# Six tile buffers instead of four, a last row tile turned by TensorE, and a check moved into the next layer, in a two-layer graph kernel

## The chip, the core and the metric

The kernel runs on one core of one Trainium2 chip. The metric is the device time of one execution in microseconds (us). The time before is the median of 3 runs.

## What is computed

The graph has 3327 nodes with 256 features each. Layer 0 does two steps. In each, it multiplies the features by a row-normalised `adj + I`, and, beside that, by a top-p attention matrix made from the features. Layer 1 is a graph attention with four heads, masked by `adj > 0`. Everything is float32. Cut to what matters here:

```
# layer 0, twice (Xa and Xf start as h = relu(layernorm(x)))
probs = softmax((Xa W1' W2') (Xa W3')')            # 3327 x 3327
keep  = the largest probs of a row until their sum reaches 0.9
A     = probs * keep, each row divided by its sum
Xf    = R Xf            # R = adj + I, rows divided by their sums
Xa    = A Xa
Z    += Xf U1[n]' + Xa U2[n]'
x = x + layernorm(h + Z)
# layer 1
hp    = relu(layernorm(x)) W                        # 4 heads of 64
attn  = softmax over j of leaky_relu(s_i + d_j), where adj[i, j] > 0
x = x + elu(attn hp)
```

## The kernel before, in words

**Tiles.** The 3327 rows are padded to 26 tiles of 128 (`NT`). In each of the two steps every tile t has two large jobs on TensorE (PE):

- The *row* job makes row tile t of the attention matrix and multiplies it. PE makes the logits (L906), ScalarE (ACT) takes their exponentials (L921), and ACT, GpSimd (POOL) and VectorE (DVE) search the threshold of each row: counting passes on ACT (L958), arithmetic on single columns on POOL (L960 to L1006), the window, sort and choice on DVE (`window`, `sort`, `choose`, L1008 to L1066). DVE then zeroes what falls below the threshold in three parts (`drop`, L1072). PE needs the row tile turned (the 128 nodes of j on the partitions). That is done in three stages: DVE turns 32 x 32 blocks (`turn_blocks`, L1084), SyncE (SP) issues a DMA that puts a part into the DRAM tensor `blocks` (`put_blocks`, L1088), and four DMAs fetch it back with the blocks in their new places (`get_blocks`, L1093). PE multiplies (`attend_blocks`, L1100, 26 products into the one bank `acca`), and ACT takes the result out (`attended`, L1104). In step 2, `finish2` carries the row on through two layer norms to layer 1's `hp`.
- The *full* job multiplies tile t of `adj + I`. SP loads it in seven pieces of up to four 128 x 128 tiles (`Full.load`, L1119) into the buffers called `at`, of which there are four. POOL adds the identity to the one diagonal tile (L1132), PE multiplies (`some`, L1125, into the one bank `accf`), and ACT or DVE takes the result out.

**Layer 1** goes over four blocks of 832 columns, and in each over j = 0 to 25. SP loads the tiles of `adj` for one j into two `at` buffers (L1680), ACT makes a 0/1 mask of them (L1690, L1691), DVE makes four lots of masked exponents (L1702), PE multiplies (L1718) and sums (L1732). The exponents of j = 3, 10 and so on lie in the room of `c`, those of j = 5 and 6 in that of `rhs`. So the first can't be written before all full jobs of step 2 are done, the second not before all row jobs are. In block 0 the sums (L1732) wait for all row jobs, since they use the same two banks.

**What sets the order.** Nothing is scheduled on the chip: each engine's queue runs in program order. That order is laid out by a planner while the program is built (`Plan`, L471). Each piece of work is put into it with an engine, a duration, a *rank* (the lowest goes first among those that are ready), what it needs, buffers that it takes and gives back by name, and a *lag*: how long after its end its result is counted as there. A DMA's lag stands for its flight time. The planner runs through these numbers and writes down who goes when; a wrong lag gives no wrong result, it only puts an instruction at a place in its queue where it then waits. Six of these numbers belong to the change: the lags of `put_blocks` (8.0) and `get_blocks` (5.5) at L1527 and L1530, that of `Full.load` (4.0) at L1544, the rank of step 2's full jobs (`base + 1.0 + t`, L1969, where row jobs have `base + t`), the rank of `failures` (L1973), and the buffer counts at L867.

**`failures`** (L1439) is a chain of small DVE instructions over one column per tile. It notes rows for which the search failed. `judge` reads it at the very end, and the program runs a slow general version of everything if any did. No row of the profile belongs to that version.

**Room.** SBUF is full, so a buffer more here is one less elsewhere. The pool `et` has three buffers of 2048 bytes per partition. They hold small weights at the start, copies for `stats` (L826), layer 1's vectors and their products (L757, L766), and in layer 1 the masks (L1685).

Of the kernel before, what the change touches and what calls it, by code (L numbers as in the profile page):

```python
# [10 lines left out]
F32 = mybir.dt.float32  # L11
BF16 = mybir.dt.bfloat16
# [3 lines left out]
ALU = mybir.AluOpType  # L16
# [3 lines left out]
P = 128  # L20
# [26 lines left out]
PIECES = 16  # L47
PART = 1024
PIECE_AT = [PART * (k // 5) + 205 * (k % 5) for k in range(PIECES)] + [N]
QUANTILE = (6.4004942, -10.1694914, 9.3637353, -4.4723851)  # L50

REACH = 40.0

BUFS = dict(kk=2, e=4, sc=6, f=3, xa=2, xt=2, kq=3, ystage=2, base=1, mv=4, cum=2)

# [531 lines left out]
def fast(  # L587
# [58 lines left out]
    with ExitStack() as l0:  # L646
        wpool = l0.enter_context(tc.tile_pool(name="wpool", bufs=1))
        small = l0.enter_context(tc.tile_pool(name="small", bufs=2))
        epool = l0.enter_context(tc.tile_pool(name="epool", bufs=4))
        apool = l0.enter_context(tc.tile_pool(name="apool", bufs=4))  # L650
        etpool = l0.enter_context(tc.tile_pool(name="etpool", bufs=3))
        scr = l0.enter_context(tc.tile_pool(name="scr", bufs=1))
# [24 lines left out]

        small.tile([P, 8], F32, name="room", bufs=1)
        stat = wpool.tile([P, 2, NT], F32, name="stat")
# [20 lines left out]
        def weights():  # L700
            held = {}
            w1 = etpool.tile([P, 4, P], F32, name="et")
            w1 = w1[:, 0, :].rearrange("p (c o) -> p c o", c=2)
# [48 lines left out]
        def layer1_loads():  # L752

            late = wpool.tile([P, 2 * D + 2 * (H * FH + 2 * H)], F32, name="late")
            g_all, b_all = late[:, :D], late[:, D : 2 * D]
            wa = late[:, 2 * D :].rearrange("p (c o) -> p c o", c=2)
            a_all = etpool.tile([P, H, 2 * FH], F32, name="et")  # L757
            nc.sync.dma_start(g_all, ln_g.partition_broadcast(P))
            nc.sync.dma_start(b_all, ln_b.partition_broadcast(P))
            nc.sync.dma_start(a_all, gat_a.partition_broadcast(P))  # L760
            nc.sync.dma_start(wa[:, :, : H * FH], gat_w.rearrange("(c p) o -> p c o", p=P))
            return g_all, b_all, wa, a_all

        def layer1_scores(wa, a_all):

            prod = etpool.tile([P, 2, H, FH], F32, name="et")  # L766
            for k in range(2):
                for a in range(2):
                    V.tensor_mul(
                        prod[:, 0],  # L770
                        wa[:, k, : H * FH].rearrange("p (h f) -> p h f", h=H),
                        a_all[:, :, a * FH : (a + 1) * FH],
                    )
                    lo = H * FH + a * H
                    V.tensor_reduce(wa[:, k, lo : lo + H], prod[:, 0], AX.X, ALU.add)

# [34 lines left out]
        def stats(n, lo, hi, rank, needs, scaled):  # L811
# [13 lines left out]
            def copy(held, m):  # L825
                qg = etpool.tile([P, 4, P], F32, name="et").rearrange("p a b -> p (a b)")  # L826
                held["qg"] = qg[:, : 3 * (2 * DA + 1)].rearrange("p (a b) -> p a b", a=3)
                S.copy(held["qg"][:, :m, :], held["ps"][:, :m, :])
# [10 lines left out]
            for t0 in range(lo, hi, 2):  # L839
                held, m = {}, min(2, hi - t0)  # L840
                a = plan.put("PE", 0.25 * m, rank, product, held, t0, m, needs=[needs, scaled], take=["px"])
                a = plan.put("ACT", 0.45, rank, copy, held, m, needs=[a], take=["et"], give=["px"])
                ends.append(plan.put("DVE", 0.35 * m + 0.2, rank, square, held, t0, m, needs=[a], give=["et"]))

# [21 lines left out]

        plan = Plan(dict(rows=1, mvs=3, pl=2, px=2, acca=1, accf=1, et=3, at=4, y=1, e2=2, ec=1, mask=2, e5=1, qg=2, **BUFS))  # L867
        own_e = [[("e", "e5")[i % 5 == 2 - n] for i in range(NT)] for n in range(STEPS)]
# [3 lines left out]
        class Row:  # L872
# [42 lines left out]
            def exps(self, k):  # L915
                pl = self.pl.pop(k)
                to, m = self.e[:, PART * k : min(PART * (k + 1), NP)], pl.shape[1]
                sums = (self.p0, self.p1, self.p2, self.p3)
                to = to.rearrange("p (g q t) -> p g t q", q=P, t=2)
                if k < 3:  # L920
                    S.activation(to, pl.rearrange("p (g t q) -> p g t q", g=4, t=2), AF.Exp, accum_out=sums[k])  # L921
                else:
                    S.activation(to[:, 0, 0, :], pl[:, :P], AF.Exp, accum_out=self.p3)
                    S.activation(to[:, 0, 1, : m - P], pl[:, P:], AF.Exp, accum_out=self.p4)

            def row_sum(self):
                k = self.NAMES.index("p4")
                S.activation(self.sc[:, k + 5 : k + 10], self.sc[:, k : k + 5], AF.Copy, accum_out=self.s)

# [144 lines left out]
            def total(self):  # L1074

                GP.tensor_scalar(self.v, self.all, self.zs, self.rec, ALU.subtract, ALU.add)
                GP.tensor_tensor(self.rec, self.v, powers[:, 2:3], ALU.pow)

            def part(self, g):
# [440 lines left out]
        def attention(row, rank, total, drops, right):  # L1520
            a = None
            come = []
            for g in range(3):
                b = plan.put(
                    "DVE", 1.17 if g < 2 else 1.44, rank - 1.001, row.turn_blocks, g, needs=[drops[g]]
                )
                b = plan.put("SP", 0.5, rank - 1.0, row.put_blocks, g, needs=[b], lag=8.0)  # L1527
                b = plan.put("", 0.0, -90.0, lambda: None, needs=[b], lag=0.0)
                come.append(
                    [plan.put("SP", 0.6, rank - 1.0, row.get_blocks, g, o, needs=[b], lag=5.5) for o in range(4)]  # L1530
                )
            for j in range(0, NT - 2, 4):
                js = range(j, j + 4 if j < 20 else NT)
                a = plan.put(
                    "PE", 0.432 * len(js), rank, row.attend_blocks, js, needs=[come[j // 8], a, right],
                    take=["acca"] * (j == 0), give=[own_e[row.n][row.i]] * (j == 20),
                )
            return plan.put("ACT", 0.4, rank - 2.7, row.attended, needs=[a, total], take=["xa"], give=["acca", "sc"])

        def full(n, t, rank, right, after):  # L1540

            f = Full(n, t)
            loads = [
                plan.put("SP", 0.4, rank, f.load, q, needs=[after], take=["at"], lag=4.0) for q in range(-(-NT // JC))  # L1544
            ]
# [19 lines left out]
        def attend_neighbours(rows, ends, done, fulls):  # L1565
# [80 lines left out]
            for b in range(4):  # L1646
# [11 lines left out]

                seen, last_acc, last_den, last_e = [], None, None, None
                group, halves = [], [None, None]  # L1660
                for j in range(NT):
# [21 lines left out]

                    def mask(held=held, off=off):
                        m = etpool.tile([P, 4, P], F32, name="et").rearrange("p a b -> p (a b)").bitcast(BF16)  # L1685
                        m = held["mask"] = m[:, :W]
                        A, B = (held.pop(g).rearrange("p i q -> p (i q)") for g in range(2))
                        A, B = A[:, off:], B[:, : W + off - 4 * P]
                        for to, src in ((m[:, : 4 * P - off], A), (m[:, 4 * P - off :], B)):
                            S.activation(src, src, AF.Relu)  # L1690
                            S.activation(to, src, AF.Sign)  # L1691
# [48 lines left out]

                    own = ["et", "mask"]
                    if b == 0 and j < 2:
                        loads, own = plan.put("SP", 0.2, rank, load_first, needs=[opened[0]], lag=4.0), []
                        m_ = plan.put("ACT", 1.8, rank, mask_first, needs=[loads])
                    else:
# [3 lines left out]
                        ]  # L1749
                        m_ = plan.put("ACT", 2.2, rank, mask, needs=[loads], take=own, give=["at", "at"])  # L1750
                    mine = ("e", "e", "e", "ec", "e", "e2", "e2")[j % 7]
# [191 lines left out]
        for n in range(STEPS):  # L1943
# [22 lines left out]
            if n == 0:  # L1966
                drawn[0] = rows[-1].pieces["logits"]
            fulls = [
                full(n, t, (2.0 + 1.3 * t if n == 0 else base + 1.0 + t), [p[0] for p in sources], [p[1] for p in sources] if n == 0 else loaded[0])  # L1969
                for t in range(NT)  # L1970
            ]
            done = [attention(r, base + r.i, *found[r.i], right) for r in rows]
            failed.append(plan.put("DVE", 2.95, base + NT, failures, n, needs=[[a for a, _ in found]]))  # L1973
            if n == 0:
# [21 lines left out]
                def layer1():  # L1996
# [6 lines left out]
                layer1_ready = plan.put(  # L2003
                    "DVE", 3.7, base + 5.0, lambda: layer1_scores(late["wa"], late["a"]), needs=[a], take=["et"],
                    give=["et", "et"],
                )
# [74 lines left out]
```

## Time and profile before

| what | value |
|---|---|
| median of 3 runs | 2075.99 us (2071.98 to 2077.3) |
| the profiled execution, whole | 2077.04 us |
| its span in the profile | 2075.2 us |
| DVE busy | 1696.3 us (82%) |
| ACT busy | 1298.7 us (63%) |
| POOL busy | 1040.1 us (50%) |
| DMA moved | 361.61 MB, mean 174 GB/s |
| granted clock of PE, mean | 0.992 |

The profiled execution is 1.05 us longer than the median, and 1.84 us of it lie around the span. The stages follow each other like this in the trace: preparation to about 100 us; step 1 to about 790 us, where the first logits of step 2 are made, while full jobs of step 1 run on to 909 us; step 2 to about 1600 us; layer 1 to the end.

How to read the lines below. A line of a PE timeline gives the start, the time from there to the end of a run of like instructions, the line of the program, the output and inputs, the number of records, and in brackets how long PE had been idle before it and who released it. One product of 128 x 128 with 256 columns makes two records. The ends of matmuls are modelled, so neighbouring pieces overlap by some tenths. A line of a table by stages gives the stretch, its length, then for each engine the busy time and in parentheses the number of its instructions, then the granted clock of PE (1.00 is full speed), the busy share of the DMA engines, and GB/s.

### The profile page before, as it was taken

The page shows a single profiled execution, that of the slowest core. Times are in us where ns is not written, and L with a number is a line of the kernel's source. Part 1 is how long each engine was busy: PE and PEld are TensorE (multiplying, and loading weights), DVE is VectorE, ACT ScalarE, POOL GpSimd, SP SyncE. Part 2 cuts the span into 40 slices and gives each one's busy share as a digit, 9 for nine tenths or more (in the row PEclk, how much of TensorE's full clock was granted, in tenths as well). Part 3 has the DMA queues.
Part 4 walks back from the last instruction along what each step waited for, and adds up shares of the span by engine and source line. Part 5 has one row for each costly group of instructions (what it writes and reads, how often), then busy time and mean ns, then how long its engine had stood idle before and what let it go on. Part 6 is the DMA issues. An engine that isn't in the chain of part 4 may idle for free. (4 is left out here: it accounts for less than half of the span.)

```text
span 2075.2 us, 33982 instructions
## 1 busy us (share of the span) xinstructions
PE 2025.6 (98%) x10519; PEld 1401.3 (68%) x10519; DVE 1696.3 (82%) x3768; ACT 1298.7 (63%) x2630; POOL 1040.1 (50%) x2222
## 2 busy tenths in 40 slices
PE   8999999999999999999999999999998999999997
PEld 6477777878787776788888788778876333333332
DVE  5479989887997742888679888898888999999894
ACT  4677685677756405884677777877643456474642
POOL 5367676665765503787576777878771000000001
PEclk9999999999999999999999999999999999999999
DMA  3177677776786756687757777676786444444440
GB/s 96 38 209 192 188 203 216 194 196 190 198 220 193 209 151 181 199 220 216 196 156 216 202 199 201 192 206 184 214 251 200 117 132 140 140 132 116 117 123 26
DMA packets 637551, 361.61 MB, mean 174 GB/s; under 512 B 373706, under 2 KB 590320, under 8 KB 637360
## 3 DMA queue, kind: packets, MB, share of 16 engines
q1 hardware_dynamic: 636464, 359.13, 61.9%
q8 instruction: 86, 1.41, 0.3%
q14 instruction: 105, 0.86, 0.1%
q10 hardware_dynamic: 896, 0.21, 0.0%
HBM read 254.39 MB, written 104.58 MB: 173 GB/s over the span
## 5 line engine op out<-in xcount | busy, mean ns | idle before, releaser
L1100 PE MATMUL acca<-rhs,e 128*128 128x256 f32 x2184 | 485.6, 380 | 4.1 <-DMA e<-blocks 2.3
L958 ACT ACTIVATE junk<-e,sc 128x3327 fp8e5<-128x3327 f32 x147 | 450.8, 3066 | 39.7 <-POOL sc L995 38.2
L1100 PEld LDWEIGHTS acca<-rhs,e 128*128 128x128 f32 x2184 | 427.9, 197 | 49.4 <-issue 3.5
L1125 PE MATMUL accf<-main,at 128*128 128x257 f32 x1352 | 323.8, 389 | 14.1 <-DMA at<-in_adjt_dram 7.6
L1125 PE MATMUL accf<-c,at 128*128 128x256 f32 x1352 | 308.6, 382 | 5.9 <-DMA at<-in_adjt_dram 2.2
L1125 PEld LDWEIGHTS accf<-main,at 128*128 128x128 f32 x1352 | 253.4, 193 | 76.6 <-issue 19.0
L1125 PEld LDWEIGHTS accf<-c,at 128*128 128x128 f32 x1352 | 252.4, 190 | 57.1 <-issue 8.9
L1021 DVE MAX8 cands<-y 128x8 f32<-128x205 f32 (+1 forms) x832 | 242.7, 362 | 3.7
L1016 DVE SCALAR_TENSOR_TENSOR y<-e,sc 128x1639 f32<-128x1639 f32 x84 | 167.5, 1994 | 65.4 <-POOL sc L1006 64.4
L1881 POOL TENSOR_TENSOR qq<-qq 128x256 f32<-128x256 f32 x4 | 2.9, 730 | 431.6 <-ACT qq L1877 431.5
L1691 ACT ACTIVATE et<-at 128x448 bf16<-128x448 f32 (+1 forms) x204 | 112.2, 550 | 128.6 <-DVE e L1702 73.4
L1718 PE MATMUL pl<-e,main 128*64 128x416 f32 x1024 | 191.6, 517 | 0.0
L921 ACT ACTIVATE e<-pl 128x1024 f32<-128x1024 f32 x126 | 137.8, 1101 | 64.5 <-PE pl L906 54.7
L906 PE MATMUL pl<-kt,qg 64*128 64x512 f32 (+1 forms) x832 | 174.0, 536 | 2.4 <-ACT e L921 2.4
L1084 DVE STREAM_TRANSPOSE e<-e 128x1024 f32<-128x1024 f32 (+1 forms) x126 | 168.7, 1339 | 7.1 <-DVE e L1072 0.5
L1072 DVE SCALAR_TENSOR_TENSOR e<-e,thr 128x1024 f32<-128x1024 f32 (+1 forms) x126 | 170.7, 1354 | 1.5 <-issue 0.4
L1718 PEld LDWEIGHTS pl<-e,main 128*64 128x64 f32 x1024 | 69.3, 137 | 109.8 <-issue 93.7
L1690 ACT ACTIVATE at<-at 128x448 f32<-128x448 f32 (+1 forms) x204 | 110.6, 542 | 45.5 <-DMA at<-in_adjt_dram 45.4
L1702 DVE SCALAR_TENSOR_TENSOR e<-c,low,et 128x832 f32<-128x832 f32 x128 | 129.4, 1071 | 8.1 <-issue 6.2
L906 PEld LDWEIGHTS pl<-kt,qg 64*128 64x128 f32 x832 | 71.4, 186 | 88.3 <-issue 74.1
L1702 DVE SCALAR_TENSOR_TENSOR e<-qq,low,et 128x832 f32<-128x832 f32 x120 | 121.4, 1076 | 8.2 <-ACT at L1690 4.3
L1104 ACT ACTIVATE xa<-acca,sc 128x256 f32<-128x256 f32 x52 | 24.3, 467 | 151.3 <-PE acca L1100 151.2
(547 smaller groups left out, 3454.2 us busy)
## 6 DMA issues: line engine op xcount, KB each, us to landing
at<-in_adjt_dram SPq DMA_DIRECT2D x414, 256.0 KB
blocks<-e SPq DMA_DIRECT2D x84, 512.0 KB
e<-blocks SPq DMA_DIRECT2D x336, 128.0 KB
blocks<-e SPq DMA_DIRECT2D x42, 640.0 KB
e<-blocks SPq DMA_DIRECT2D x168, 160.0 KB
at<-in_adjt_dram SPq DMA_DIRECT2D x102, 192.0 KB
blocks<-qq SPq DMA_DIRECT2D x20, 512.0 KB
qq<-blocks SPq DMA_DIRECT2D x80, 128.0 KB
```

The source lines that it names most:

```text
L906: T.matmul(pl[:, lo : lo + m], qg[self.n, self.i // 4][half, self.i % 4, :], kt[half, 512 * k : 512 * k + m], start=True, stop=True,)
L921: S.activation(to, pl.rearrange("p (g t q) -> p g t q", g=4, t=2), AF.Exp, accum_out=sums[k])
L958: S.activation(junk[:, :N], self.e[:, :N], fn, bias=t, scale=-1.0, accum_out=dst, saturate=False)
L1016: V.scalar_tensor_tensor(self.y[:, : hi - lo], self.e[:, lo:hi], self.up, self.e[:, lo:hi], ALU.is_lt, ALU.mult, accum_out=(self.h0, self. ...
L1021: V.max(self.cands[:, a * PIECES // 2 + k, :], self.y[:, at[k] - lo : at[k + 1] - lo])
L1072: V.scalar_tensor_tensor(piece, piece, self.thr[:, at : at + 1], piece, ALU.is_gt, ALU.mult)
L1084: V.transpose(part, part)
L1100: T.matmul(self.acc, lhs, rhs[self.n][:, j, :], start=(j == 0), stop=(j == NT - 1))
L1125: T.matmul(self.acc[:, : self.w], self.at[j // JC][:, j % JC, :], self.src[:, j, : self.w], start=(j == 0), stop=(j == NT - 1),)
L1691: S.activation(to, src, AF.Sign)
L1702: V.scalar_tensor_tensor(held["e"][:, k, :], extra["both"][b % 2][:, k, :], low[:, j, k : k + 1], held["mask"], ALU.max, ALU.mult,)
L1718: T.matmul(q["acc"][a][k * FH : (k + 1) * FH, c, :C], main[:, j, h * FH : (h + 1) * FH], held["e"][:, h, c * C : (c + 1) * C], start=(j == 0),
```

## The change

The change has these parts.

1. **Buffers.** `at` gets six buffers of 2048 bytes for four. The room comes from `et`, which shrinks to one buffer of 3072 bytes, and from `f`, which has two for three. `stats` now uses `f` for its copies, layer 1's vectors and their products share the one `et`, and the masks of layer 1 lie in two halves of the room called `m` (that of `junk`), where only the first two lay before.
2. **The last row tile of step 2** (tile 25 of the second step, and no other) takes another way. Its exponentials are stored in plain order. PE turns it in seven groups of up to four 128 x 128 tiles into PSUM (`turn`), ACT or DVE copies each group into an `at` buffer (`turned`), and PE multiplies from there (`attend`). This row has no `turn_blocks`, `put_blocks` or `get_blocks`.
3. **`failures` of step 2** gets rank 63.0 where it had `base + NT`, which is 56. Layer 1's block 0 has ranks from 60 on.
4. **Planner numbers.** The lag of `put_blocks` is 7.0 for 8.0, of `get_blocks` 5.0 for 5.5, of `Full.load` 5.5 for 4.0. The full jobs of step 2 have rank `base + 2.0 + 1.05 * t` for `base + 1.0 + t`.

```diff
+BLOCKED = (NT, NT - 1)
...
-BUFS = dict(kk=2, e=4, sc=6, f=3, xa=2, xt=2, kq=3, ystage=2, base=1, mv=4, cum=2)
+BUFS = dict(kk=2, e=4, sc=6, f=2, xa=2, xt=2, kq=3, ystage=2, base=1, mv=4, cum=2)
...
-        apool = l0.enter_context(tc.tile_pool(name="apool", bufs=4))
-        etpool = l0.enter_context(tc.tile_pool(name="etpool", bufs=3))
+        apool = l0.enter_context(tc.tile_pool(name="apool", bufs=6))
+        etpool = l0.enter_context(tc.tile_pool(name="etpool", bufs=1))
...
-                qg = etpool.tile([P, 4, P], F32, name="et").rearrange("p a b -> p (a b)")
-                held["qg"] = qg[:, : 3 * (2 * DA + 1)].rearrange("p (a b) -> p a b", a=3)
+                qg = small.tile([P, H * FH + 2 * H], F32, name="f", bufs=BUFS["f"])
+                held["qg"] = qg[:, : 2 * (2 * DA + 1)].rearrange("p (a b) -> p a b", a=2)
...
-        plan = Plan(dict(rows=1, mvs=3, pl=2, px=2, acca=1, accf=1, et=3, at=4, y=1, e2=2, ec=1, mask=2, e5=1, qg=2, **BUFS))
+        plan = Plan(dict(rows=1, mvs=3, pl=2, px=2, acca=1, accf=1, et=1, at=6, y=1, e2=2, ec=1, mask=2, e5=1, qg=2, **BUFS))
...
-                if k < 3:
+                if self.i >= BLOCKED[self.n]:
+                    S.activation(self.e[:, PART * k : PART * k + m], pl, AF.Exp, accum_out=sums[k])
+                elif k < 3:
...
+            def turn(self, g):
+                m = min(4, NT - 4 * g)
+                pt = self.pt[g] = ps_x.tile([P, 4, P], F32, name="px")
+                for k in range(m):
+                    j = 4 * g + k
+                    T.transpose(pt[:, k, :], self.e[:, j * P : (j + 1) * P], ident)
...
+            def turned(self, g, copy):
+                m = min(4, NT - 4 * g)
+                self.et[g] = apool.tile([P, JC, P], F32, name="at")
+                copy(self.et[g][:, :m, :], self.pt.pop(g)[:, :m, :])
+
+            def attend(self, g):
+                if g == 0:
+                    self.acc = ps_a.tile([P, D], F32, name="acca")
+                et = self.et.pop(g)
+                for j in range(4 * g, min(4 * g + 4, NT)):
+                    T.matmul(
+                        self.acc, et[:, j - 4 * g, :], rhs[self.n][:, j, :], start=(j == 0), stop=(j == NT - 1)
+                    )
...
+            if row.i >= BLOCKED[row.n]:
+                for g in range(GROUPS):
+                    m = min(4, NT - 4 * g)
+                    b = plan.put(
+                        "PE", 0.11 * m, rank - 0.01 * (GROUPS - g), row.turn, g, needs=[drops[min(((4 * g + m) * P - 1) // PART, 2)]],
+                        take=["px"], give=[own_e[row.n][row.i]] * (g == GROUPS - 1),
+                    )
+                    b = plan.either(
+                        ("ACT", 0.06 + 0.105 * m, row.turned_by_s), ("DVE", 0.12 + 0.135 * m, row.turned_by_v),
+                        rank - 2.6, g, needs=[b], take=["at"], give=["px"],
+                    )
+                    a = plan.put(
+                        "PE", 0.432 * m, rank, row.attend, g, needs=[b, a, right], take=["acca"] * (g == 0), give=["at"]
+                    )
+                return plan.put("ACT", 0.4, rank - 2.7, row.attended, needs=[a, total], take=["xa"], give=["acca", "sc"])
...
-                b = plan.put("SP", 0.5, rank - 1.0, row.put_blocks, g, needs=[b], lag=8.0)
+                b = plan.put("SP", 0.5, rank - 1.0, row.put_blocks, g, needs=[b], lag=7.0)
...
-                    [plan.put("SP", 0.6, rank - 1.0, row.get_blocks, g, o, needs=[b], lag=5.5) for o in range(4)]
+                    [plan.put("SP", 0.6, rank - 1.0, row.get_blocks, g, o, needs=[b], lag=5.0) for o in range(4)]
...
-                plan.put("SP", 0.4, rank, f.load, q, needs=[after], take=["at"], lag=4.0) for q in range(-(-NT // JC))
+                plan.put("SP", 0.4, rank, f.load, q, needs=[after], take=["at"], lag=5.5) for q in range(-(-NT // JC))
...
-                    def mask(held=held, off=off):
-                        m = etpool.tile([P, 4, P], F32, name="et").rearrange("p a b -> p (a b)").bitcast(BF16)
-                        m = held["mask"] = m[:, :W]
+                    def mask(j=j, held=held, off=off):
+                        m = held["mask"] = extra["m"][:, j % 2, :]
...
-                        m_ = plan.put("ACT", 2.2, rank, mask, needs=[loads], take=own, give=["at", "at"])
+                        m_ = last_m = plan.put("ACT", 2.2, rank, mask, needs=[loads, last_m], take=own, give=["at", "at"])
...
-                full(n, t, (2.0 + 1.3 * t if n == 0 else base + 1.0 + t), [p[0] for p in sources], [p[1] for p in sources] if n == 0 else loaded[0])
+                full(n, t, (2.0 + 1.3 * t if n == 0 else base + 2.0 + 1.05 * t), [p[0] for p in sources], [p[1] for p in sources] if n == 0 else loaded[0])
...
-            failed.append(plan.put("DVE", 2.95, base + NT, failures, n, needs=[[a for a, _ in found]]))
+            failed.append(plan.put("DVE", 2.95, base + NT if n == 0 else 63.0, failures, n, needs=[[a for a, _ in found]]))
```

More of the change, by code (lines that the diff above doesn't have):

```diff
@@ L676, in fast @@
             GP.tensor_copy(gk[:DA, DA + 1 :], ident[:DA, :DA])
-        small.tile([P, 8], F32, name="room", bufs=1)
+        small.tile([P, 16], F32, name="room", bufs=1)
         stat = wpool.tile([P, 2, NT], F32, name="stat")
@@ L701, in weights @@
             held = {}
-            w1 = etpool.tile([P, 4, P], F32, name="et")
+            w1 = etpool.tile([P, 3 * D], F32, name="et")[:, : 4 * P].rearrange("p (a b) -> p a b", a=4)
             w1 = w1[:, 0, :].rearrange("p (c o) -> p c o", c=2)
@@ L756, in layer1_loads @@
             wa = late[:, 2 * D :].rearrange("p (c o) -> p c o", c=2)
-            a_all = etpool.tile([P, H, 2 * FH], F32, name="et")
+            a_all = etpool.tile([P, 3 * D], F32, name="et")
+            prod = a_all[:, 2 * D :].rearrange("p (h f) -> p h f", h=H)
+            a_all = a_all[:, : 2 * D].rearrange("p (h f) -> p h f", h=H)
             nc.sync.dma_start(g_all, ln_g.partition_broadcast(P))
@@ L761, in layer1_loads @@
             nc.sync.dma_start(wa[:, :, : H * FH], gat_w.rearrange("(c p) o -> p c o", p=P))
-            return g_all, b_all, wa, a_all
+            return g_all, b_all, wa, (a_all, prod)
         def layer1_scores(wa, a_all):
-            prod = etpool.tile([P, 2, H, FH], F32, name="et")
+            a_all, prod = a_all
             for k in range(2):
@@ L769, in layer1_scores @@
                     V.tensor_mul(
-                        prod[:, 0],
+                        prod,
                         wa[:, k, : H * FH].rearrange("p (h f) -> p h f", h=H),
@@ L774, in layer1_scores @@
                     lo = H * FH + a * H
-                    V.tensor_reduce(wa[:, k, lo : lo + H], prod[:, 0], AX.X, ALU.add)
+                    V.tensor_reduce(wa[:, k, lo : lo + H], prod, AX.X, ALU.add)
         def moments(n, t, kq, ps_k, ps_g):
@@ L841, in stats @@
                 a = plan.put("PE", 0.25 * m, rank, product, held, t0, m, needs=[needs, scaled], take=["px"])
-                a = plan.put("ACT", 0.45, rank, copy, held, m, needs=[a], take=["et"], give=["px"])
-                ends.append(plan.put("DVE", 0.35 * m + 0.2, rank, square, held, t0, m, needs=[a], give=["et"]))
+                a = plan.put("ACT", 0.45, rank, copy, held, m, needs=[a], take=["f"], give=["px"])
+                ends.append(plan.put("DVE", 0.35 * m + 0.2, rank, square, held, t0, m, needs=[a], give=["f"]))
             def variance():
@@ L926, in row_sum @@
             def row_sum(self):
-                k = self.NAMES.index("p4")
-                S.activation(self.sc[:, k + 5 : k + 10], self.sc[:, k : k + 5], AF.Copy, accum_out=self.s)
+                m = 5 if self.i < BLOCKED[self.n] else 4
+                k = self.NAMES.index("p0") + 1
+                S.activation(self.sc[:, k + 5 - m : k + 5], self.sc[:, k - m : k], AF.Copy, accum_out=self.s)
             def root(self):
@@ L1077, in total, with turned_by_s, turned_by_v @@
                 GP.tensor_tensor(self.rec, self.v, powers[:, 2:3], ALU.pow)
+            def turn(self, g):
[4 more added lines that the diff above has]
+                    T.transpose(pt[:, k, :], self.e[:, j * P : (j + 1) * P], ident)
+            def turned_by_s(self, g):
+                self.turned(g, S.copy)
+            def turned_by_v(self, g):
+                self.turned(g, V.tensor_copy)
+            def turned(self, g, copy):
[10 more added lines that the diff above has]
+                    )
             def part(self, g):
@@ L1657, in open_den @@
                     q["den"] = [ps_a.tile([P, 512], F32, name=n) for n in ("acca", "accf")]
-                seen, last_acc, last_den, last_e = [], None, None, None
+                seen, last_acc, last_den, last_e, last_m = [], None, None, None, None
                 group, halves = [], [None, None]
@@ L1739, in sums @@
                                 )
-                    own = ["et", "mask"]
+                    own = ["mask"]
                     if b == 0 and j < 2:
-                        loads, own = plan.put("SP", 0.2, rank, load_first, needs=[opened[0]], lag=4.0), []
-                        m_ = plan.put("ACT", 1.8, rank, mask_first, needs=[loads])
+                        loads = plan.put("SP", 0.2, rank, load_first, needs=[opened[0]], lag=4.0)
+                        m_ = last_m = plan.put("ACT", 1.8, rank, mask_first, needs=[loads, last_m], take=own)
                     else:
@@ L2003, in fast @@
                 layer1_ready = plan.put(
-                    "DVE", 3.7, base + 5.0, lambda: layer1_scores(late["wa"], late["a"]), needs=[a], take=["et"],
-                    give=["et", "et"],
+                    "DVE", 3.7, base + 5.0, lambda: layer1_scores(late["wa"], late["a"]), needs=[a], give=["et"],
                 )
```

## The prediction

> **What bounds the kernel now.** I read the page first, then a table by stages, then PE's timeline around each stage where PE was not full, then what the other engines did there.
>
> ```profile
> PE 2025.6 (98%) x10519; PEld 1401.3 (68%) x10519; DVE 1696.3 (82%) x3768; ACT 1298.7 (63%) x2630; POOL 1040.1 (50%) x2222
> PE   8999999999999999999999999999998999999997
> ```
>
> PE is the bound: 49.6 us of 2075.2 are idle. No part of the change takes work from PE, so the most it can win is idle time and what follows from it. The table says where that is:
>
> ```profile
> 0.00:101.00 101.00, 90.73 (x384) 55.02 (x385) 50.72 (x191) 59.04 (x150) 42.49 (x136) 0.97 0.23 66
> ...
> 700.00:800.00 100.00, 89.94 (x390) 72.93 (x389) 45.71 (x137) 18.75 (x36) 19.98 (x41) 0.95 0.65 180
> ...
> 1150.00:1500.00 350.00, 345.88 (x1607) 281.67 (x1606) 302.62 (x766) 264.60 (x509) 275.91 (x591) 1.00 0.73 199
> 1500.00:1605.00 105.00, 94.48 (x441) 73.53 (x441) 88.83 (x192) 47.06 (x91) 53.59 (x96) 0.97 0.79 228
> 1605.00:2020.00 415.00, 415.00 (x3033) 151.78 (x3031) 394.53 (x450) 231.14 (x564) 3.74 (x3) 1.00 0.44 127
> 2020.00:2076.00 56.00, 44.60 (x314) 13.77 (x309) 27.52 (x41) 13.11 (x30) 5.34 (x7) 0.92 0.11 32
> ```
>
> The head (10.3) and the tail (about 10.6 to the end of the span) are not touched. Layer 1 has no PE idle time at all. What is left are two passages: from step 1 to step 2 (10.1 idle in 700 to 800, clock 0.95) and from step 2 to layer 1 (10.5 in 1500 to 1605, clock 0.97), and some 7 us scattered elsewhere. PE's timeline names the waits:
>
> ```profile
> 748.45 2.01 PE L1125 MATMUL accf<-main,at 128*128 128x257 f32 x8 [0.73 <-DMA at<-in_adjt_dram]
> 753.11 3.69 PE L1125 MATMUL accf<-main,at 128*128 128x257 f32 x8 [2.66 <-DMA at<-in_adjt_dram]
> 756.63 11.39 PE L1100 MATMUL acca<-rhs,e 128*128 128x256 f32 x52
> ...
> 785.54 5.40 PE L1125 MATMUL accf<-main,at 128*128 128x257 f32 x12 [4.17 <-DMA at<-in_adjt_dram]
> ```
>
> ```profile
> 1519.47 0.70 PE L1125 MATMUL accf<-c,at 128*128 128x256 f32 x2 [2.15 <-POOL at L1132]
> 1521.29 3.58 PE L1100 MATMUL acca<-rhs,e 128*128 128x256 f32 x8 [1.12 <-DVE y L1016]
> ...
> 1588.71 4.48 PE L1100 MATMUL acca<-rhs,e 128*128 128x256 f32 x20
> 1593.12 1.62 PE L1718 MATMUL pl<-e,main 128*64 128x416 f32 x8
> 1599.27 1.30 PE L1732 MATMUL acca<-e,qd 128*32 128x416 f32 x8 [4.54 <-ACT xa L1104]
> ```
>
> Eight records of L1125 take 2.01 us, but 3.69 after the gap at 753: the gap costs twice, once idle and once in a slow clock (granted 0.50 to 0.57 from 753 to 756, 0.50 from 784 to 790 in slices of 1 us).
>
> **Part 1, six `at` buffers (passage 1).** A buffer is 4 tiles of work: 1.75 us of PE (11.39 for 26). Four hold 7.0, six 10.5, so 3.5 more. Whether the two more would be full is read from the stretch ahead: PE spends 724 to 736 and 757 to 768 on a row job (52 records each), which frees no `at` buffer, and in 5 us slices the DMA share falls to 0.12 and 0.31 (730 to 740), and 0.01 and 0.03 (760 to 770), with SP's next load held back by PE (L1119 <- PE accf, 18.7 us in 700 to 800). So the two loads fall into idle DMA time and push nothing. They cover 0.73 + 2.66 whole and 3.5 of the 4.17: 6.9. Clock: 3.69 against 2.01 is 1.7; 12 records in 5.40 against 2.88 is 2.5; together 4.2.
>
> Here the Trainium skill, "TensorE: Matmul & The Clock Gate" (Part 1), would give less: it says that the clock halves after an idle window of about 3.4 us. By that rule only the 4.17 gap pays (2.5). The rows show that 2.66, and 2.15 and 1.12 with 0.7 of work between, pay too, so I use the rows. Full gain 6.9 + 4.2 = 11.1. Bounds 0 (the row's twelve fetches, which have DMA at a share of 1.0 from 745 to 757, are what binds) and 12. I take 8, since part of the work moved forward meets the next wait, such as a fetch of `rhs`.
>
> The same buffers cover the scattered waits for tiles in step 2 (1.34, 0.35 and 0.22): 1.5.
>
> **What pays for the buffers.** `f` and `et` lose one and two. `stats` is 13 copies per step, each held until a DVE instruction is done, about 1 us; a full job's copy of step 1 that met two of them would hold `accf` by that. PE waits for that copy 1.7 us in all now; bounds 0 and +2, taken 0.5. The masks lose nothing: two were allowed before (`mask`=2), two halves are there now. A half is written while the other is read; that parts of one buffer don't wait for each other is seen at 1535 to 1541, where DVE goes on with parts 1 and 2 of a row while the put of part 0 is in flight.
>
> **Part 2, the last row by TensorE (passage 2).** Removed: three turns on DVE (1.25 + 1.25 + 1.52 = 4.0), three puts and twelve gets, whose issues take 11.2 us of SP's queue (0.38, 0.39, 0.46; 4.62, 2.37, 2.94) and move 3.3 MB, 14.6 us of DMA at this stage's 228 GB/s. Added: 26 transposes and seven copies of 512 columns. Two transposes of L1401 stand 0.22 apart from what follows, so 26 are 2.9 us, and PE is the bound, so they count whole. The skill speaks against this one: the same page (Part 4, PE-mode transpose) says that full clock does not engage for transposes and that they don't count as busy. By that they would take 5.7 and leave PE slow behind. The start of this trace says otherwise:
>
> ```profile
> 1.79 4.14 PE L1922 MATMUL accf<-ident 128*128 128x128 f32 x19 [1.79 <-POOL ident masks.py:199]
> 5.77 0.43 PE L1211 MATMUL pl<-ident,rhs 128*128 128x128 f32 x2
> 6.03 0.82 PE L1922 MATMUL accf<-ident 128*128 128x128 f32 x6
> ```
>
> All of these are transposes: 0.218 each at first, 0.11 to 0.14 after 4 us of nothing else. They do raise the clock. I take 2.9 (bounds 2.9 and 5.7). The copies: 0.37 for 256 columns (ACT, L1405) makes an estimated 0.65 for 512, 4.5 in all, on an ACT that waits 11.04 us at 1564 and is busy 47 of 105 here; taken at nothing, at worst 0.7 per group not overlapped, 4.5. The plain exponentials are four ACT instructions of 1.1 us as before (bounds -0.3 and +0.3).
>
> What it wins: the last drop ends at 1568.5, or about 1566 without the turns between, and PE now begins the last row at 1579.7 and its last part at 1588.7. With seven groups of 0.44 (PE) and 0.65 (ACT), the whole row is there by about 1569. PE gets it before the last full job, which becomes the filler while DVE makes layer 1's first exponents. Its `attended` then no longer queues on ACT behind the mask that waits from 1591.9 to 1596.7 for tiles. So 4.54 goes, and the slow clock behind it (32 records of L1732 in 4.6 us against 2.8): 6.3.
>
> The 2.15 and 1.12 at 1519 belong to a diagonal tile and to the search of a late row. Two loads further ahead bring the diagonal earlier, but POOL's queue also holds single-column work; I count half of 3.3 + 1.7, so 2.5 (bounds 0 and 5). The four waits of 0.56 to 0.64 for `accf`, `acca` and ACT stay.
>
> **Part 3, `failures`.** 16 instructions, 3.1 us of DVE (1575.4 to 1578.6), move from passage 2 into block 0. There DVE needs 4.03 per j (8.05 for 8 instructions) and PE 4.33, and at 1611 DVE is two j ahead, 8 us. 3.1 fits in that lead; without it, up to 3.1 on the path. Taken 0. In passage 2 it gives DVE room, which the 6.3 above uses.
>
> **Part 4, the lags and ranks.** They cost no instruction; they lay out the whole order anew, on SP, PE, ACT, DVE and POOL. Lag 5.5 for tiles follows what the trace shows late (9.8 us of PE waits for `at`), and the blocks' lags are shortened where little is late: PE waits for `e` or `qq` <- blocks 2.9 us in all, in 3 of 156 groups. Full jobs one to two ranks later leave PE about one full job (11.4) more to fill passage 2 with. Bounds: -3 and +25 (third rival); taken +2.
>
> **Sum**, against the profiled execution: -8 - 1.5 + 0.5 + 2.9 - 6.3 - 2.5 + 2 = -12.9, so 2077.0 - 12.9 = 2064.1. The median is 1.05 below that execution: 2063.
>
> **The rivals.**
> 1. *One passage only* (chance 0.16). Passage 2 is set by the row search, whose chain DVE, POOL, ACT ends at 1568 whatever PE does; then what PE wins in passage 1 is waited for at the end. For it: ACT waits for POOL and POOL for ACT throughout (63.5 + 48.3 us). Against: DVE is busy 303 of 350 in 1150 to 1500, so rows could go faster than PE takes them. Only the last row's own delay is won: -6.3 - 2.5 + 2.9 = -5.9, 2070; a little more or less puts it at either side of 0.3%.
> 2. *Hidden anyway* (0.08). In passage 1 DMA is at a share of 1.0 just where PE waits; more loads in flight slow the blocks by as much, and the transposes eat a part of passage 2: 2074.
> 3. *The new order is worse* (0.14), slower. The plan now counts 12 us for a row's way through `blocks` (7 + 5) where it counted 13.5. If the flight takes more than that, PE comes to a group too early and stands, with the full jobs queued behind it. Were one group in 6 of the 156 to wait 0.9 us (the mean of the three now is 1.0), that is 23 us: 2063 + 23 = 2086. It decides from 13 us, which is 0.08 per group. Against: SP never waits for a put before a get now, so 8.0 was loose.
>
> **How the numbers follow.** The forecast (0.62) is 2063. A change is told from none from 0.3%, 6.2 us. Faster is the forecast and most of rival 1 (0.12): 0.74. Same is the rest of it (0.04) and rival 2: 0.12. Slower is rival 3: 0.14. The low end takes all gains full: -12 - 1.5 + 2.9 - 6.3 - 5 - 3 is -24.9, 2051. The high end reaches past rivals 1 and 2 to 2078.
>
> **What would show it.** Right: in passage 1 no wait for `at` above 1 us and no stretch at clock 0.50; L1125 waits for DMA in all below 4; no 4.5 us before the first L1732; transposes at 0.11; the first L1732 some 12 us earlier. Wrong: PE waits for blocks of 10 us and more (rival 3), new waits for the rows between 800 and 1500, PE waiting for DVE early in layer 1, or a second passage that ends late for want of row 25.

## The result, and the profile after

The changed kernel takes 2056.29 us (median of 4 runs, 2055.5 to 2058.27), the one before 2073.98 beside it. The ratio is 0.9924, 95% interval 0.9912 to 0.9937: faster by 17.7 us, where 13 were forecast, and inside the range. The two profiled executions are 2077.04 and 2056.36 us, spans 2075.2 and 2054.5: 20.7 apart.

The page of the changed kernel, first the engines, then PE's slices:

```profile
PE 2019.0 (98%) x10545; PEld 1397.3 (68%) x10545; DVE 1691.5 (82%) x3753; ACT 1301.6 (63%) x2647; POOL 1029.3 (50%) x2222
PE   8999999999999999999999999999999999999997
```

PE has 26 instructions more (the transposes) and is busy 6.6 us less. The slice that stood at 8 is full. PE's idle time falls from 49.6 to 35.5. So 14.1 of the 20.7 is idle time, and 6.6 is PE being quicker at more work. The same stages as before:

```profile
150.00:650.00 500.00, 497.61 (x2284) 392.32 (x2284) 427.86 (x1068) 339.16 (x643) 310.26 (x668) 1.00 0.71 198
...
700.00:800.00 100.00, 99.07 (x460) 82.02 (x459) 54.38 (x169) 28.68 (x55) 25.58 (x59) 1.00 0.73 207
...
950.00:1150.00 200.00, 196.99 (x918) 160.12 (x918) 164.07 (x430) 144.07 (x287) 140.26 (x309) 1.00 0.69 190
1150.00:1500.00 350.00, 345.22 (x1598) 281.17 (x1595) 294.38 (x739) 259.72 (x500) 274.50 (x581) 1.00 0.72 200
1500.00:1605.00 105.00, 103.70 (x571) 73.35 (x570) 89.25 (x185) 43.14 (x91) 45.21 (x73) 1.00 0.64 185
1605.00:2020.00 415.00, 415.00 (x3041) 150.95 (x3039) 400.50 (x456) 230.23 (x564) 3.72 (x3) 1.00 0.42 124
```

Both passages are closed: 0.9 us idle in 700 to 800 (10.1 before) and 1.3 in 1500 to 1605 (10.5 before), and the granted clock is 1.00 in both. The middle of the steps got a little worse: 2.4 idle for 0.8 in 150 to 650, and 3.0 in 950 to 1150, where there was none. Around the last row, PE's timeline (lines have new numbers: L1090 is `turn`, L1108 `attend`, L1133 `attend_blocks`, L1158 the full jobs, L1765 and L1779 the products and sums of layer 1):

```profile
1557.50 1.04 PE L1090 MATMUL px<-ident,e 128*128 128x128 f32 x8
1558.38 3.62 PE L1158 MATMUL accf<-c,at 128*128 128x256 f32 x16
1561.83 0.60 PE L1090 MATMUL px<-ident,e 128*128 128x128 f32 x4
1562.27 1.89 PE L1108 MATMUL acca<-rhs,at 128*128 128x256 f32 x8
...
1576.14 2.75 PE L1158 MATMUL accf<-c,at 128*128 128x256 f32 x12
1578.83 1.62 PE L1765 MATMUL pl<-e,main 128*64 128x416 f32 x8
1580.37 0.91 PE L1779 MATMUL acca<-e,qd 128*32 128x416 f32 x8
```

There is no bracket on any of these lines: PE goes from the turned row and the last full job into layer 1 without a wait. Four transposes take 0.44 us (1561.83 to 1562.27). The first sums start at 1580.4 instead of 1599.3.

### The profile page after: what moved, and what is told of

The parts are those of the page before. It is cut to its first block, busy times and chain, and to the rows that moved or that the text cites. A ratio compares the mean times of both kernels' runs of the same rounds, so it can differ in the third digit from the quotient of the medians.

```text
span 2054.5 us, 34072 instructions
## 1 busy us (share of the span) xinstructions
PE 2019.0 (98%) x10545; PEld 1397.3 (68%) x10545; DVE 1691.5 (82%) x3753; ACT 1301.6 (63%) x2647; POOL 1029.3 (50%) x2222
## 5 line engine op out<-in xcount | busy, mean ns | idle before, releaser
L1133 PE MATMUL acca<-rhs,e 128*128 128x256 f32 x2132 | 471.9, 380 | 3.6 <-DMA e<-blocks 3.5
L1133 PEld LDWEIGHTS acca<-rhs,e 128*128 128x128 f32 x2132 | 416.5, 196 | 50.2 <-issue 6.9
L1158 PE MATMUL accf<-main,at 128*128 128x257 f32 x1352 | 316.4, 383 | 7.4 <-ACT f L1169 2.6
L1158 PE MATMUL accf<-c,at 128*128 128x256 f32 x1352 | 308.4, 382 | 4.5 <-DVE main L1175 3.7
L1158 PEld LDWEIGHTS accf<-main,at 128*128 128x128 f32 x1352 | 249.9, 190 | 66.4 <-issue 18.9
L1158 PEld LDWEIGHTS accf<-c,at 128*128 128x128 f32 x1352 | 252.6, 190 | 54.0 <-issue 9.4
L1738 ACT ACTIVATE junk<-at 128x448 bf16<-128x448 f32 (+1 forms) x204 | 112.2, 550 | 178.1 <-DVE e L1749 109.3
L1765 PE MATMUL pl<-e,main 128*64 128x416 f32 x1024 | 192.2, 517 | 0.0
L1117 DVE STREAM_TRANSPOSE e<-e 128x1024 f32<-128x1024 f32 (+1 forms) x123 | 164.5, 1338 | 7.2 <-POOL sc L1004 0.5
L1765 PEld LDWEIGHTS pl<-e,main 128*64 128x64 f32 x1024 | 69.0, 137 | 109.5 <-issue 91.7
L1749 DVE SCALAR_TENSOR_TENSOR e<-qq,low,junk 128x832 f32<-128x832 f32 x128 | 129.5, 1076 | 4.4 <-ACT junk L1738 2.8
L1749 DVE SCALAR_TENSOR_TENSOR e<-c,low,junk 128x832 f32<-128x832 f32 x128 | 129.1, 1071 | 4.2 <-issue 3.2
L1133 PE MATMUL acca<-rhs,qq 128*128 128x256 f32 x520 | 115.0, 380 | 0.3 <-DVE thr L1069 0.3
```

The costliest lines, as they stand in the source:

```text
L1117: V.transpose(part, part)
L1133: T.matmul(self.acc, lhs, rhs[self.n][:, j, :], start=(j == 0), stop=(j == NT - 1))
L1158: T.matmul(self.acc[:, : self.w], self.at[j // JC][:, j % JC, :], self.src[:, j, : self.w], start=(j == 0), stop=(j == NT - 1),)
L1749: V.scalar_tensor_tensor(held["e"][:, k, :], extra["both"][b % 2][:, k, :], low[:, j, k : k + 1], held["mask"], ALU.max, ALU.mult,)
L1765: T.matmul(q["acc"][a][k * FH : (k + 1) * FH, c, :C], main[:, j, h * FH : (h + 1) * FH], held["e"][:, h, c * C : (c + 1) * C], start=(j == 0),
```

## The experiments

All are told by the ratio to the kernel before on the same chip, since chips differ by some us. 0.3% is 6.2 us.

| label | at buffers | rank of full jobs | lags | last row | ratio (95%) | median us |
|---|---|---|---|---|---|---|
| the change | 6 | later | new | TensorE | 0.9924 (0.9912 to 0.9937) | 2056.3 |
| no_turn | 6 | later | new | blocks | 0.9957 (0.9941 to 0.9973) | 2064.1 |
| four_bufs | 4 | later | new | TensorE | 1.0119 (1.0101 to 1.0136) | 2099.3 |
| early_check | 6 | later | new | TensorE | 0.9922 (0.9903 to 0.994) | 2059.0 |
| old_numbers | 6 | old | old | TensorE | 0.9999 (0.9988 to 1.0009) | 2072.1 |
| rank_back | 6 | old | new | TensorE | 0.9983 (0.9972 to 0.9994) | 2068.0 |
| lags_back | 6 | later | old | TensorE | 0.9895 (0.9873 to 0.9916) | 2050.3 |
| four_bufs_lag4 | 4 | later | blocks new, tiles old | TensorE | 1.0056 (1.0034 to 1.0079) | 2085.6 |
| bufs_alone | 6 | old | old | blocks | 1.0006 (0.9992 to 1.002) | 2073.6 |
| rank_alone | 4 | later | old | blocks | 1.0088 (1.0071 to 1.0105) | 2089.3 |
| bufs_rank | 6 | later | old | blocks | 0.9954 (0.9937 to 0.997) | 2060.4 |
| tile_lag_kept | 6 | later | blocks old, tiles new | TensorE | 0.9911 (0.9894 to 0.9927) | 2051.3 |
| later_still | 6 | one more | old | TensorE | 0.9911 (0.9894 to 0.9927) | 2051.7 |

The first theory was the prediction's: each part mends its own passage, and the parts add up. The rival: the lags and ranks do it.

**no_turn**, the last row through the blocks again.

```diff
-BLOCKED = (NT, NT - 1)
+BLOCKED = (NT, NT)
```

> The changed kernel (2056.3), with the last row of step 2 sent through DVE and the DRAM blocks again. Theory A (each part mends its own passage): the wait of about 4.5 us ahead of the first L1732-type sum comes back with its slow clock, 2.9 us of transposes go, so about +3.5: 2060, and the passage from step 1 to step 2 stays as it is. Theory B (the new lags and ranks do the work, by another order): no more than +1: 2057.

Measured 0.9957: 0.33% given back, 7 us (profiled: 3.9). The wait is there again, at another place, on PE's timeline:

```profile
1571.11 10.57 PE L1133 MATMUL acca<-rhs,e 128*128 128x256 f32 x40 [4.53 <-DMA e<-blocks]
```

It is 4.53 us, and a slow stretch follows: 40 records in 10.57 us, where 40 of the same kind take 8.80 in the changed kernel. The rest is like there. So the last row's part is as forecast in kind; its size is 3.9 by the profiled executions, 7 by the ratio, where +3.5 was expected.

**four_bufs**, the buffers taken back alone.

```diff
-        apool = l0.enter_context(tc.tile_pool(name="apool", bufs=6))
+        apool = l0.enter_context(tc.tile_pool(name="apool", bufs=4))
...
-et=1, at=6,
+et=1, at=4,
```

> The changed kernel with four tile buffers instead of six, all else kept. Theory A: the waits for tiles from 745 to 786 come back, 7 us idle and 4 of slow clock, with 1.5 elsewhere: 2068. Theory B: the longer lag for tiles lays the order out for late tiles, so at most 3 us come back: 2059.

Measured 1.0119, 43 us above the change and worse than the kernel before. Neither theory had that. PE is idle 67.6 us instead of 35.5. It waits for tiles 19.7 us in 13 places, 11 of them between 790 and 1605.

**early_check**, `failures` at its old rank.

```diff
-base + NT if n == 0 else 63.0, failures
+base + NT, failures
```

> The changed kernel with the failures check of step 2 at its old rank, so that its 3.1 us of DVE lie at the end of step 2 again. Theory A: DVE has idle time there now, so nothing: 2056, 2058 at most. Theory B': the room on DVE is what lets layer 1's first exponents come in time, so the whole 3.1 comes back: 2059.

Measured 0.9922, no difference that can be told. The trace shows why it could not matter: in the changed kernel the chain starts at 1557.3 us, here at 1561.4. That is ahead of the last row's products in both, so the check did not move into the next layer at all. In the planner a rank only decides among what is ready at the time, and DVE has little ready there: in the changed kernel it is busy 7.1 us of the 20 from 1560 to 1580.

**old_numbers**, the three lags and the rank put back.

```diff
-row.put_blocks, g, needs=[b], lag=7.0)
+row.put_blocks, g, needs=[b], lag=8.0)
...
-needs=[b], lag=5.0) for o in range(4)]
+needs=[b], lag=5.5) for o in range(4)]
...
-take=["at"], lag=5.5) for q in
+take=["at"], lag=4.0) for q in
...
-base + 2.0 + 1.05 * t)
+base + 1.0 + t)
```

> The changed kernel with the old planner numbers (lags 8.0, 5.5 and 4.0, rank base + 1 + t). Theory A: the buffers and the last row do nearly all, so about +2: 2058, with the passages still closed. Theory B: most of the gain goes, 2068, and the end of step 2 has 5 us and more of PE waits again, since no full job is left to fill it.

Measured 0.9999: the whole gain is gone, with six buffers and the last row by TensorE still in place. Passage 1 is closed (99.07 of 100). Passage 2 has this:

```profile
1523.34 7.93 PE L1133 MATMUL acca<-rhs,e 128*128 128x256 f32 x36
1531.11 1.89 PE L1158 MATMUL accf<-c,at 128*128 128x256 f32 x8
1555.52 3.75 PE L1133 MATMUL acca<-rhs,e 128*128 128x256 f32 x8 [22.52 <-DMA e<-blocks]
```

By 1533 the last full job is done. The second to last row still has its way through DVE and DRAM ahead of it, and PE stands 22.5 us. SP's queue shows that row's puts at 1529 to 1535 and its fetches from 1541 on. So the first theory fell: the passages are not independent. What PE wins early it waits for at the end, unless there is work left to fill it. The next two runs separate rank from lags.

**rank_back** has only the last of these lines put back, **lags_back** only the first three.

> The changed kernel (2056.3) with only the rank of step 2's full jobs put back to base + 1 + t; the new lags stay. Theory A' (after the last four runs): the later rank is what keeps full jobs back to fill the end of step 2, so the wait of some 20 us for the blocks of a late row comes back: 2070. Theory L (the lags do it): no such wait, 2058.

> The changed kernel with only the three lags put back (8.0, 5.5, 4.0); the later rank stays. Theory A': 2057 to 2060, both passages closed. Theory L: 2070, with a long wait at the end of step 2.

Measured 0.9983 and 0.9895. It is the rank: with the old one, a single wait of 13.32 us stands in passage 2, ahead of the second to last row's products. PE's line in rank_back, and one of SP's:

```profile
1552.12 9.35 PE L1133 MATMUL acca<-rhs,e 128*128 128x256 f32 x32 [13.32 <-DVE rest L1046]
```

```profile
1543.77 7.90 SPq L1126 DMA_DIRECT2D e<-blocks  x8
```

The profile puts the wait down to a DVE instruction that ends just then, but that one belongs to the sort of the last row; the row that PE waits for has its fetches on SP's queue from 1543.8 to 1551.7, and PE starts at 1552.1, so it is most likely the blocks again. With the new rank and the old lags the kernel is faster than the change itself, and below both of its expectations. So beside the new lags the rank is worth 0.59% (12 us), and beside the new rank the new lags cost 0.29% (6 us, with intervals that just overlap). These two don't add up to the whole: beside the old lags the rank is worth 1.04% (old_numbers against lags_back, 22 us).

**bufs_alone**: the buffers and the moved room, everything else as before the change (the edits of no_turn, early_check and old_numbers together).

> Six buffers and the moved room alone: rank, lags, way of the last row and rank of the check as before the change. Theory A': the passage from step 1 to step 2 closes (11 us), but full jobs then run out sooner and the end of step 2 waits for rows by as much: 2070 to 2074, no gain that counts. Theory P (each passage by itself, as in the prediction): 2074 less 8 and 1.5: 2064.

Measured 1.0006. Of its table by stages, the two passages:

```profile
700.00:800.00 100.00, 99.07 (x462) 81.34 (x461) 50.25 (x159) 37.43 (x61) 31.27 (x69) 1.00 0.71 204
...
1500.00:1605.00 105.00, 78.49 (x384) 57.05 (x382) 88.31 (x177) 38.48 (x76) 43.93 (x78) 0.85 0.71 198
```

and of its PE timeline the line that explains it:

```profile
1554.30 3.75 PE L1133 MATMUL acca<-rhs,e 128*128 128x256 f32 x8 [23.57 <-DMA e<-blocks]
```

The buffers do in passage 1 all that was asked of them: 0.9 idle for 10.1. And passage 2 loses 26.5 where it lost 10.5, in idle time, and its mean clock goes to 0.85, most of that inside the wait. No run moves the room alone, but it costs nothing that can be seen: PE waits 3.1 us for copies into `f`, which has one buffer less (3.3 before).

**rank_alone**: the later rank without the buffers (four buffers, old lags, blocks, early check). **four_bufs_lag4**: the changed kernel with four buffers and the tiles' lag of 4.0.

> The later rank of step 2's full jobs and the moved room alone: four buffers, old lags, the last row through the blocks, the check early. Theory A'' (rank and buffers are worth something only together): the waits for tiles between the steps stay, and four buffers are short for the later order, as in the other two runs with four (2099 and 2086): 2080 or more. Theory R (the rank is the gain): 2060.

> The changed kernel with four tile buffers and the old lag of 4.0 for tiles; rank, block lags, last row and check stay. Theory A' (the longer lag is what four buffers can't carry: the planner then holds every full job back): the 43 us of the run with four buffers mostly go, what stays is the waits for tiles between the steps, 11 us, and 2 elsewhere: 2069. Theory F (four buffers alone are too few for the later order): 2090 or more, with waits for tiles throughout step 2.

Measured 1.0088 and 1.0056, slower than before. The old tile lag takes back part of the loss (43 us became 29), not most: both expectations of four_bufs_lag4 hold in part. With the later rank, full jobs run in turn with row jobs up to the end, and four buffers fail at some of these turns as they failed in passage 1 (17.0 us of waits for tiles in 8 places in rank_alone, 9.8 in 7 before). PE's timeline of rank_alone, and two of its 5 us slices:

```profile
1517.43 11.47 PE L1133 MATMUL acca<-rhs,e 128*128 128x256 f32 x52 [0.55 <-DMA e<-blocks]
1528.74 6.21 PE L1158 MATMUL accf<-c,at 128*128 128x256 f32 x28
1541.31 2.07 PE L1158 MATMUL accf<-c,at 128*128 128x256 f32 x4 [6.36 <-DMA at<-in_adjt_dram]
```

```profile
1525.00:1530.00 5.00, 5.00 (x25) 4.52 (x24) 4.57 (x20) 4.22 (x4) 3.79 (x10) 1.00 0.10 31
...
1535.00:1540.00 5.00, 0.00 (x0) 0.00 (x0) 3.30 (x3) 0.00 (x0) 3.22 (x7) 0.95 0.92 351
```

A row job of 11.5 us frees no buffer, DMA falls to 0.10, then PE eats what four buffers hold in 6.2 us, and the next tiles, requested from 1531 on behind other transfers, are there at 1541.

**bufs_rank**: six buffers and the later rank, nothing else.

> Six buffers and the later rank; old lags, the last row through the blocks, the check early. Theory A'': both passages but for the last row's own delay, so the run with the lags back (2050.3) plus the 4 to 8 us that taking the last row back cost there, plus 0 to 3 for the check: 2054 to 2061, clearly under both parts alone. If they merely add up (nothing by the buffers, the rank as measured alone), it lies with the run of the rank alone.

Measured 0.9954. The one alone 1.0006, the other alone 1.0088, both together 0.9954: they are worth something only together. With the last row's way and the check (lags_back) it is 0.9895, so the last row is worth 0.6% here. Its wait in this run is 5.53 us for the blocks, at 1566.9. It needs the later rank too: with the old one, the last row's way and the check together gained nothing (old_numbers 0.9999, bufs_alone 1.0006).

**tile_lag_kept**: the changed kernel with only the two block lags put back.

> The changed kernel with the lags of the two block transfers back (8.0 and 5.5) and the tiles' lag of 5.5 kept. With all three back it took 2050.3, with none 2056.3. If the shorter block lags cost the 6 us (PE comes to blocks too early, the prediction's third rival in small): 2050. If the longer tile lag does (the planner lets PE stand where a tile is there in truth): 2056.

Measured 0.9911. That lies between the change (0.9924) and lags_back (0.9895), and its interval overlaps both. The profiled spans speak against the block lags: 2047.1, with all three lags back 2047.9, in the changed kernel 2054.5. But these are single executions, and chips differ by some us. So it is likely that the shorter block lags cost, and not the tiles' lag, but it isn't shown. PE waits for blocks 3.5 us in 6 places in the changed kernel (the longest 1.68, at 1101) and 1.0 us in 2 with the lags back. That is 2.5 of the 6.6 between the two spans. The rest is spread over waits of half a microsecond and over the clock, and which of them the lags caused stays open.

**later_still**: lags back, and `base + 3.0 + 1.05 * t`.

> All three lags back, and the full jobs of step 2 one rank later still (base + 3.0 + 1.05 t). If filling the end of step 2 is all that the rank does, and 2.4 us of waits are left there, 2049 to 2050. If full jobs held back longer put row and full jobs out of step, or delay layer 1's first exponents (j = 3 needs all of them): 2055 and more, with PE waits around 1570.

Measured 0.9911: no better than lags_back, which fits an end that is already filled. The lowest median of this study is that of lags_back, 2050.3 us; tile_lag_kept and later_still can't be told from it.

## Why the prediction was right, and where it was not

- **Part 1, the buffers.** Mechanism and place right: the waits for `at` in passage 1 went from 7.6 us to none of size, and no stretch at half clock is left. It was sized at 8. Passage 1 won 9.1 us of idle time and, by the rows the prediction used, 4.2 of clock; with the waits for tiles alone (7.6) that is 11.8, over the full 11.1. "Part of the work moved forward meets the next wait" was true, but of passage 2, not of a fetch of `rhs`. The scattered waits for tiles (1.5) went to 0.2 in all. The cost of the room, +0.5, did not show: waits for copies into `f` grew by 1.6 us in the changed kernel (4.9 for 3.3) but not in bufs_alone (3.1), so they seem to come with the new order, not with the room.
- **Part 2, the last row.** Right in mechanism, but only beside the later rank (bufs_rank and lags_back); with the old one it gained nothing. The 4.54 is gone, 26 transposes take 2.9 us (four in 0.44 us) at a granted clock of 1.00, and putting the row back cost 3.9 to 7 us against a net of 3.4 in the sum (6.3 less 2.9). The copies take 0.585 us on ACT, estimated at 0.65, and no PE wait names one. The half of the waits at 1519 that was counted went, and so did the other half. The first sums came 18.9 us earlier, where some 12 were named.
- **Part 3, `failures`.** The cost of nothing was right, the reason wrong. It was said to move into block 0 and lean on DVE's lead there; it stayed in step 2. The rank was read as a place in time.
- **Part 4, the lags and ranks.** This is the failed term: +2 in the sum. Taking the whole part back (old_numbers) gives back 0.75%, 15.6 us, all of the gain. It holds two terms of opposite sign, the rank at -12 to -22 and the lags at +6, and their sizes depend on each other: with the old rank the new lags don't cost (rank_back 0.9983, old_numbers 0.9999). The text saw that the later rank leaves "about one full job (11.4) more to fill passage 2 with", and gave it no number. The third rival's mechanism, PE meeting blocks too early, does exist: 3.5 us of waits where there were 2.9, far below the 13 from which it would have decided.
- **The sum.** It added the passages as if each were paid for by itself. bufs_alone shows that they aren't: by that sum it had to be 2064, and it was no faster than before. The first rival described that give-back. It is what happens without the rank, and the rank is why it didn't. So it is in part luck that 2063 came near 2056: without part 4, all that the sum counted as gain came to nothing (old_numbers), and the part that it put at a cost of 2 made the difference.

## What to carry to other kernels

On a chain that ends in a drain, a stall removed early is only kept if there is other work to put where the drain stands: look at what is late next before counting the gain. Here two parts that each gained nothing or lost alone (1.0006 and 1.0088) made more than half of the change's gain together (0.46% of 0.76%), so take parts back one by one as well as adding them one by one. A buffer count can't be read from the mean rate. After a row job, in which nothing is freed for 11.4 us and DMA runs dry, the full buffers have to carry PE until the next load has landed. In rank_alone that load took some 10 us (1531.2 to 1541.3); four buffers hold 7.0 us of work and six 10.5, an estimate from 1.75 us for each.

## What the runs showed of the hardware that was not expected

After a longer wait PE often runs at half clock for a while, so that the wait costs more than its length. Its length alone does not tell whether it does. The changed kernel and early_check differ only in a rank of step 2. At about 98 us both wait 2.37 us at the same place; the first goes on at full clock, the second takes 8.85 us for what took 7.22 (granted 0.50 from 98 to 100). First the changed kernel, then early_check:

```profile
97.77 7.22 PE L1158 MATMUL accf<-main,at 128*128 128x257 f32 x32 [2.37 <-DVE cands L1027]
97.45 8.85 PE L1158 MATMUL accf<-main,at 128*128 128x257 f32 x32 [2.37 <-DVE cands L1027]
```

So a single execution can be 1.6 us slower by this alone. The slow stretches of all these traces, but for those that the end of the kernel cuts off, last 3.4 us or a multiple of it (3.4, 6.8, 13.7, 23.9, 27.3). A wait of ten times the length costs little more clock than a short one. After the 2.66 us wait of before, PE worked 3.4 us at half clock; after the 22.5 us of old_numbers 4.6, and after the 23.6 us of bufs_alone 5.9. The rest of the slow stretch lay inside the wait.

Between the two kernels, PE is busy 6.6 us less with 2.9 us of transposes more, so an estimated 9.5 us of the 20.7 were slow clock. The rows of the prediction show 7.7 of it. Another 1.7 is a slow stretch at 98 us in the trace of before, after a wait of 2.73 us; no part of the change was meant for it, and the pair of lines above shows that such a stretch can come or not after the same wait.
